# An attention and mixture-of-experts kernel on one core: output weights in eight pieces, a third query buffer, and late loads on ScalarE's queue

## Chip, cores and metric

The kernel runs on 1 core of one Trainium2 chip. The metric is the device time of one execution in microseconds, the median of three runs. Engines are named as the profile names them: PE (matrix products), DVE (VectorE), ACT (ScalarE), POOL (GpSimd) and SP (SyncE, which here only issues DMAs).

## What is computed

One layer for 2048 rows of 256 features: attention with 16 heads of 128 and weights stored as codes and block scales, then a mixture of 8 experts of width 176, two of them chosen for each row. Cut to what matters:

```
x = x + layernorm(attention(layernorm(x)))
x = x + layernorm(experts(layernorm(x)))

attention(x): w  = codes * repeat(scales, 32)          # for wq, wk, wv, wo
              q, k, v = x @ wq + bq, x @ wk + bk, x @ wv + bv
              out = softmax(q k^T / sqrt(128)) v       # each of 16 heads, 2048 x 2048
              return out @ wo + bo
experts(x):   top 2 of softmax(x @ Wr), weights normalised
              sum over them of weight * ((silu(x @ Wg) * (x @ Wu)) @ Wd)
```

## The kernel before, in words

All engines run one instruction list each, in the order in which the Python code calls them (a manual schedule); nothing is reordered. Numbers are held as a 16-bit high part and a low part, so most products run as three.

**The main loop** (L832 to L889) runs over 256 tiles `g`, 16 tiles `t` of 128 query rows for each of 16 heads `h`. In a tile, PE makes the scores of 128 queries with 2048 keys in two halves `s` (L511 to L515, 12 matmuls of 512 columns), DVE takes their maxima (`m`, L516, and L520), ACT the exponentials (`p`, L527). One tile later ACT scales `p` to the high part `ph` (L541) and SP issues its transpose by DMA to `pth`; DVE makes the low part `pl` in two halves (L556), one of them two tiles later, and SP issues the transpose to `ptl`. PE multiplies the transposed parts with `v` in units of 6 matmuls (`pv`, L582), two units a tile, 13 units behind. After eight units ACT, POOL and POOL's DMA queue write a block of 512 queries to the scratch `ot_d` in HBM (L597 to L602).

**Filling work** (`fill`, L610) puts projections into the tiles: a block of q or k in even tiles, v in odd ones. PE writes them to the single PSUM buffer `pj`, ACT copies them out (L246, L277), POOL splits them in two parts (L247, L248, L278, L279). In the first six tiles of head 0 the v blocks of the first pair of heads use the buffer `pv` and are split by ACT and DVE (L269, L270). A q block serves four tiles; it lies in a buffer `qT` of which there are 2. In the last head the three remaining q blocks are made at tiles 0, 1 and 2, the last two into slots of the pool (`qT_l`).

**One pool of slots.** `NX = 21` slots of 4 KB a partition under the tag `x` hold `ph`, `pl`, the k and v tiles, the raw and finished output weights, attention output read back (`oi`), raw expert weights (`gu_raw`, `draw`), inputs (`x1`) and more. A tile takes the slot that was given up first, and whoever writes it first waits until its last reader is done; for `pl` that is the DMA of its transpose.

**Output weights.** Codes (`woc`) and scales (`wos`) come in four pieces each before the loop. `dequant_wo` (L637) multiplies one piece on POOL in each of tiles 0 to 3 of head 0 (L642, 128x1024). The results `wo` are first read in head 14.

**The last two heads.** `early` (head 14, L793) prepares the bias row (`crow`, `brow`, which share one slot) and begins to load `oi`. `late` (head 15, L810) does the first rows' output product: `OI_LOAD` names the tiles at which an `oi` is loaded, `OI_USE` those at which its 16 matmuls (L727) run; `GW_LOAD` and `GW_SPLIT` do so for the four pieces of the experts' gate weights, which ACT and POOL split (L661, L663). All these loads are issued on SP's queue, between the transposes. The gate weights' buffer takes the place of the projections' input and weights, so it is opened once the last projection is emitted.

**After the loop** (L1107 on) the last `pv` units, the rest of the first output products (`op_mm`, L712), layer norms, routing and then the experts run, a block of 512 rows after the other.

Of the kernel before, what the change touches and what calls it, by code (L numbers as in the profile page):

```python
# [8 lines left out]
F32 = mybir.dt.float32  # L9
F32R = mybir.dt.float32r  # L10
BF = mybir.dt.bfloat16
HP = mybir.dt.float16
# [3 lines left out]
ALU = mybir.AluOpType  # L16
# [5 lines left out]
D = 256  # L22
# [11 lines left out]
NX = 21  # L34
# [3 lines left out]
def sandwich(  # L38
# [22 lines left out]
    nc = tc.nc  # L61
# [45 lines left out]
    small = ctx.enter_context(tc.tile_pool(name="small", bufs=4))  # L107
# [85 lines left out]
    kqv = ctx.enter_context(tc.tile_pool(name="kqv", bufs=2))  # L193
# [20 lines left out]

    def kq_tile(which, h, b):
        if which == "q":
            return kqv.tile([128, 2, 512], HP, name="qT", bufs=2)
        if b % 2 == 0:
            KP[h] = kqv.tile([128, 2, 2, 512], HP, name="kT", tag="x", bufs=NX)
        return KP[h][:, b % 2]  # L220

    def proj_qk(which, h, b, tag="pj", wide=None, slot=None):
        w = W[(h // 2, which)]
        bias = bqs[:, IX[which], h : h + 1]
        ps = proj_psum(tag)
        col = bass.ts(h % 2, 128)
        n = 0
        for kc in range(2):
            for hl in range(2):
                nc.tensor.matmul(  # L230
                    ps, w[:, kc, col], xnT[:, 4 * b : 4 * b + 4, hl * 2 + kc, :],
                    start=(n == 0), stop=(n == 3),
                )
                n += 1
        if slot is None:
            t = kq_tile(which, h, b)
        else:
            t = kqv.tile([128, 2, 512], HP, name="qT_l", tag="x", bufs=NX)
        if wide is None:
            nc.scalar.activation(t[:, 0, :], ps, AF.Identity, bias=bias)  # L240
            pending.append(lambda: nc.vector.scalar_tensor_tensor(
                t[:, 1, :], ps, bias, t[:, 0, :], ALU.add, ALU.subtract
            ))
        else:
            t32 = wide.tile([128, 512], F32, name="t32")
            nc.scalar.activation(t32, ps, AF.Identity, bias=bias)  # L246
            nc.gpsimd.tensor_copy(t[:, 0, :], t32)  # L247
            nc.gpsimd.tensor_tensor(t[:, 1, :], t32, t[:, 0, :], ALU.subtract)  # L248
        (Q if which == "q" else K)[(h, b)] = t
# [31 lines left out]
    wo = []  # L281
    wo_raw = {}
# [291 lines left out]
    def pv_part(h, b, e):  # L574
# [11 lines left out]
        if e == 7:  # L586
# [20 lines left out]
    QK = {0: ("q", 0, 1), 2: ("k", 1, 0), 4: ("q", 0, 2), 6: ("k", 1, 1),  # L607
          8: ("q", 0, 3), 10: ("k", 1, 2), 12: ("q", 1, 0), 14: ("k", 1, 3)}

    def fill(h, t):  # L610
        p = h // 2
        if h == 0 and t < 6:
            proj_v(0, 4 + 2 * t, 2, "pv")
        if h == NH - 1:
            if t < 3:
                proj_qk("q", h, t + 1, wide=soft, slot="x" if t > 0 else None)
        elif t in QK:
            kind, dh, b = QK[t]
            if h + dh < NH:
                proj_qk(kind, h + dh, b, wide=soft)  # L620
        elif h % 2 == 0:
            if t in (3, 5) and h > 0:
                proj_v(p, 12 + (t - 3) // 2, 1, wide=soft)
            elif t == 7 and h > 0:
                proj_v(p, 14, 2, wide=soft)
            elif t >= 9 and p + 1 < NH // 2:
                proj_v(p + 1, (t - 9) // 2, 1, wide=soft)
        elif p + 1 < NH // 2:
            proj_v(p + 1, 4 + t // 2, 1, wide=soft)
# [4 lines left out]
            pv_part(n // 4, n % 4, e)  # L634


    def dequant_wo(q):  # L637
        sc, cd = wo_raw.pop(q)
        if q % 2 == 0:
            wo.append(kqv.tile([128, 8, D], BF, name="wo", tag="x", bufs=NX))  # L640
        hs = slice(4 * (q % 2), 4 * (q % 2) + 4)
        nc.gpsimd.tensor_tensor(wo[q // 2][:, hs], cd, sc, ALU.mult)  # L642

    def bias_row():
        pb = psA.tile([128, 512], F32, name="pb", tag="pj")
# [21 lines left out]
    def load_gu(src, i, pool, tag, bufs, eng=None):  # L667
        kc, eh = divmod(i, 2)
        stg = pool.tile([128, 4, I], F32, name="gu_raw", tag=tag, bufs=bufs)
        (eng or nc.sync).dma_start(  # L670
            out=stg,
            in_=src.rearrange("e (kc p) i -> kc p e i", p=128)[kc][:, 4 * eh : 4 * eh + 4],
        )
        return stg
# [11 lines left out]
    def load_oi(b, half, j, tag="x", eng=None):  # L686
        oi = kqv.tile(
            [128, 4, 2, 256], HP, name="oi", tag=tag, bufs=NX
        )
        (eng or nc.sync).dma_start(  # L690
            out=oi.rearrange("p h l q -> p (h l q)"),
            in_=ot_d[b][:, half, 4 * j : 4 * j + 4].rearrange("p h l q -> p (h l q)"),
        )
        OIN[(b, half, j)] = oi
# [82 lines left out]
    def ln_c(b):  # L777
# [1 line left out]

    X1 = {}  # L780
    XV = x.rearrange("b (c p t) d -> p (b c) t d", p=128, t=4)
    GW_LOAD = {0: 1, 3: 2, 5: 3}
    GW_SPLIT = {4: 0, 6: 1, 8: 2, 10: 3}
    OI_LOAD = {
        2: (0, 1, 0), 4: (0, 1, 1), 6: (0, 1, 2), 9: (1, 0, 0), 10: (1, 0, 1),
        12: (0, 0, 3), 13: (0, 1, 3), 14: (1, 0, 2),
    }
    OI_USE = {
        4: (0, (0,)), 5: (0, (1,)), 6: (0, (2,)), 8: (1, (0,)), 9: (1, (1,)), 10: (1, (2,)),
        14: (0, (3,)), 15: (1, (3,)),  # L790
    }

    def early(t):  # L793
        nonlocal crow, brow
        if t == 7:
            cb = kqv.tile([128, 2, D], F32, name="crow", tag="x", bufs=NX)
            crow, brow = cb[:, 0], cb[:, 1]
            nc.sync.dma_start(out=brow, in_=bo.partition_broadcast(128))
        if t == 9:
            gst["b3"] = bias_row()  # L800
        if t == 11:
            bias_row2(gst.pop("b3"))
        if t == 13:
            nc.gpsimd.tensor_tensor(crow, crow, brow, ALU.add)
        if t in (8, 10, 12):
            load_oi(0, 0, t // 2 - 4)
        if t == 14:
            gst[0] = load_gu(wg, 0, kqv, "x", NX)

    def late(t):  # L810
        nonlocal gw
        if t == 3:
            proj_ctx.close()
            rp = ctx.enter_context(tc.tile_pool(name="gw", bufs=1, side="right"))
            gw = rp.tile([128, 2, 2, NCH, 128], F32R)
        if t in OI_USE:
            op_mm(0, *OI_USE[t], "pj", 2)
        if t in GW_SPLIT:
            split_gu(gw, GW_SPLIT[t], gst.pop(GW_SPLIT[t]), True)
        if t in GW_LOAD:  # L820
            i = GW_LOAD[t]
            gst[i] = load_gu(wg, i, kqv, "x", NX)
        if t in OI_LOAD:
            load_oi(*OI_LOAD[t])
        if t == 8:
            X1[0] = kqv.tile([128, 4, D], F32, name="x1_0", tag="x", bufs=NX)
            nc.sync.dma_start(out=X1[0], in_=XV[:, 0])


    defer = False  # L830
# [1 line left out]
    for g in range(NS + 2):  # L832
        h, t = divmod(g, NT)
        live = g < NS
        if live:
            m = small.tile([128, 8], F32, name="m", bufs=6)
            s0 = scores_half(h, t, 0, m)
            if g == 0:
                proj_v(0, 0, 2)
                proj_v(0, 2, 2, "pv")  # L840
        if prev is not None:
            recip(prev[2])
        if prev2 is not None:
            low_half(1, *prev2)
        flush()
        if defer:
            pv_unit(2 * g - 1)
            defer = False
        pv_unit(2 * g)
        if prev is not None:  # L850
            prev = (*prev, high_part(*prev))
        if live:
            s1 = scores_half(h, t, 1, m)
            negmax(m)
            p = softmax((s0, s1), m)
        if prev is not None:
            low_half(0, *prev)
        prev2 = prev
        first = live and (2 * g + 1 - PVLAG) % 8 == 0
        if not first:  # L860
            pv_unit(2 * g + 1)
        if live:
            fill(h, t)
        if first and h == NH - 1:
            defer = True
        elif first:
            pv_unit(2 * g + 1)
        if live:
            prev = (h, t, m, p)
        else:  # L870
            prev = None
        if live:
            weight_steps(h, t)
        if h == 0 and t in (8, 9):
            tail_consts(t - 8)
        if g < 4:
            dequant_wo(g)
        if h == NH - 2:
            early(t)
        if h == NH - 1:  # L880
            late(t)
        if g == NS:
            ln_a(0)
        if g == NS + 1:
            load_oi(1, 0, 3)
            ust = [load_gu(wu, 0, kqv, "x", NX)]
            ust += [load_gu(wu, i, kqv, "x", NX) for i in range(1, 4)]
            ln_b1(0)
# [222 lines left out]
    uw = uwp.tile([128, 2, 2, NCH, 128], F32R)  # L1111
    d0 = load_d(0)
    d1 = load_d(4)
    op_mm(1, 0, (0, 1), "s")
    ln_b2(0)
    split_gu(uw, 0, ust[0], True)
    ln_c(0)
# [2 lines left out]
    tr(0, 0, "s")  # L1120
    tr(0, 1, "s")
    split_gu(uw, 1, ust[1], False)
    op_mm(1, 0, (2, 3), "s")
    for j in range(4):
        load_oi(1, 1, j)
    router_a(0, "s")
# [112 lines left out]
```

## Time and profile before

| | |
|---|---|
| three runs | 1839.41, 1842.27, 1844.51 us; median 1842.27 |
| profiled execution | 1839.29 us, span 1837.5 us |
| granted clock of PE, mean | 0.990 |
| PE, DVE, ACT, POOL busy | 1780.7, 1635.1, 1371.9, 943.3 us |
| transposes issued by SP | 2 x 256, median 2.2 us (`pth`) and 3.0 us (`ptl`) each |
| main loop | about 36 to 1566 us |
| output weight products on POOL (L642) | 4 of 2.36 us, from 41.6 us on |

Times in the profile are from the start of the span. A timeline row gives start, duration, engine, line, operation, output<-inputs and shapes; in brackets stands how long the engine was idle before it and what ended that wait. A row of one line's instructions gives their number, then the shortest, median and longest duration in ns, and when the first and last began. A matmul of 512 columns starts every 0.22 us when PE runs at its full clock, though each shows 0.38 us. SP's rows are the issuing of a DMA, not its transfer.

### The profile page before, as it was taken

The numbers are of one execution on the slowest core, as the hardware profiler recorded it, in microseconds if no ns is written. First come the engines' busy times: TensorE is split into PE (matmuls) and PEld (weight loads), VectorE is DVE, ScalarE is ACT, GpSimd is POOL, SyncE is SP. The second block draws the span as 40 slices with busy tenths as digits, with TensorE's granted clock in tenths as the row PEclk, the third lists the DMA queues.
The fourth block names the chain that finished last, engine by engine and source line by source line (L and its number), as shares of the span: only waits on it lengthen the run. The fifth ranks groups of instructions, "written<-read, shape, count | busy, mean of one in ns | idle before, by whom it ended". The sixth has DMA issues, their size and how long they took to land. (4 is left out here: it accounts for less than half of the span.)

```text
span 1837.5 us, 25510 instructions
## 1 busy us (share of the span) xinstructions
PE 1780.7 (97%) x8890; PEld 936.4 (51%) x8890; DVE 1635.1 (89%) x2269; ACT 1371.9 (75%) x1732; POOL 943.3 (51%) x911
## 2 busy tenths in 40 slices
PE   7699999999999999999999999999999999899997
PEld 4344444444444444444444444444444444588886
DVE  7899999999999999999999999999999978558665
ACT  5688888888888888888888888888888877322232
POOL 3456556565656565656565656566444332323232
PEclk9899999999999999999999999999999999999999
DMA  7799999999999999999999999999999999921000
GB/s 172 136 196 203 199 199 199 203 202 189 200 207 193 201 198 208 194 200 198 199 199 198 204 205 202 194 205 198 191 190 194 216 217 227 310 83 35 1 13 23
DMA packets 1092336, 330.70 MB, mean 180 GB/s; under 512 B 1069728, under 2 KB 1079280, under 8 KB 1092208
## 3 DMA queue, kind: packets, MB, share of 16 engines
q1 hardware_dynamic: 1081744, 301.02, 89.8%
q0 software_dynamic: 9920, 27.82, 5.7%
q8 instruction: 70, 1.15, 0.2%
q14 instruction: 58, 0.48, 0.1%
q10 hardware_dynamic: 544, 0.23, 0.0%
HBM read 41.68 MB, written 18.87 MB: 33 GB/s over the span
## 5 line engine op out<-in xcount | busy, mean ns | idle before, releaser
L527 ACT ACTIVATE p<-s,m,ssc 128x1024 f32<-128x1024 f32 x512 | 612.2, 1200 | 182.7 <-DVE m L520 176.0
L556 DVE SCALAR_TENSOR_TENSOR pl<-p,m,ph 128x1024 f16<-128x1024 f32 x512 | 730.3, 1426 | 9.1 <-ACT ph L541 7.0
L516 DVE TENSOR_REDUCE m<-s 128x1 f32<-128x1024 f32 x512 | 622.0, 1215 | 37.1 <-PE s L515 34.9
L541 ACT ACTIVATE ph<-p,m 128x2048 f16<-128x2048 f32 x256 | 512.8, 2003 | 62.3 <-ACT t L246 17.3
L582 PE MATMUL pv<-pth,v 128*128 128x512 f16 x2048 | 506.3, 380 | 10.5 <-issue 5.1
L582 PEld LDWEIGHTS <-v 128*128 128x128 f16 x3072 | 301.0, 98 | 378.1 <-issue 10.0
L511 PE MATMUL s<-kT,qT 128*128 128x512 f16 x992 | 377.3, 380 | 5.9 <-ACT p L527 5.2
L512 PE MATMUL s<-kT,qT 128*128 128x512 f16 x992 | 377.2, 380 | 0.0
L515 PE MATMUL s<-kT,qT 128*128 128x512 f16 x992 | 296.0, 380 | 0.0
L582 PE MATMUL pv<-ptl,v 128*128 128x512 f16 x1024 | 253.1, 380 | 0.0
L247 POOL CAST qT<-t 128x512 f16<-128x512 f32 x61 | 76.4, 1252 | 231.7 <-ACT t L246 231.7
L278 POOL CAST v<-t 128x256 f16<-128x256 f32 (+1 forms) x105 | 44.0, 419 | 256.8 <-ACT t L277 256.8
L279 POOL TENSOR_TENSOR v<-t,v 128x256 f16<-128x256 f32 (+1 forms) x105 | 163.0, 1552 | 8.5
L515 PEld LDWEIGHTS <-qT 128*128 128x128 f16 x992 | 97.3, 98 | 118.0 <-issue 1.6
L512 PEld LDWEIGHTS <-qT 128*128 128x128 f16 x992 | 97.3, 98 | 114.0 <-issue 11.6
L511 PEld LDWEIGHTS <-qT 128*128 128x128 f16 x992 | 97.3, 98 | 106.3 <-issue 2.2
L1004 POOL TENSOR_TENSOR hh<-sg,hh 128x512 fp32r<-128x512 f32 x42 | 55.1, 1311 | 143.4 <-ACT hh L1003 108.4
L1003 ACT CAST hh<-sg 128x512 fp32r<-128x512 f32 (+1 forms) x45 | 27.5, 611 | 107.1 <-DVE sg L1015 107.0
L527 ACT ACTIVATION_READ_ACCUMULATOR p<-s,m,ssc 128x1 f32 x512 | 99.0, 193 | 0.0
L599 POOL TENSOR_TENSOR o<-t,o 128x512 f16<-128x512 f32 x63 | 93.6, 1486 | 5.2
L247 POOL CAST kT<-t 128x512 f16<-128x512 f32 x60 | 64.8, 1080 | 60.3 <-ACT t L246 56.5
L258 PE MATMUL pj<-wv,xnT 128*128 128x256 bf16 x512 | 75.9, 277 | 16.2 <-DVE v L270 16.1
(197 smaller groups left out, 1894.7 us busy)
## 6 DMA issues: line engine op xcount, KB each, us to landing
oi<-ot_d SPq DMA_DIRECT2D x32, 512.0 KB, 5.5
ot_d<-o POOLq DMA_DIRECT2D x63, 256.0 KB, 4.5
pth<-ph SPq DMA_TRANSPOSE x256, 5.1
ptl<-pl SPq DMA_TRANSPOSE x256, 5.4
xt<-in_L_attn_x SPq DMA_DIRECT2D x4, 512.0 KB, 4.2
woc<-in_L_attn_wo_codes SPq DMA_DIRECT2D x4, 512.0 KB, 8.7
wos<-in_L_attn_wo_scales SPq DMA_DIRECT2D x16, 128.0 KB, 8.1
x<-in_L_attn_x SPq DMA_DIRECT2D x4, 512.0 KB, 5.0
```

The source lines that it names most:

```text
L247: nc.gpsimd.tensor_copy(t[:, 0, :], t32)
L258: nc.tensor.matmul(ps[:, bass.ts(j, 256)], xnT[:, t0 + j, hl * 2 + kc, :], w[:, kc, :], start=(i == 0), stop=(i == 3),)
L279: nc.gpsimd.tensor_tensor(v[:, 1, sl, :], t32, v[:, 0, sl, :], ALU.subtract)
L511: nc.tensor.matmul(s[:, j, :], q[:, 0, qc], k[:, 0, :], start=True, stop=False)
L512: nc.tensor.matmul(s[:, j, :], q[:, 0, qc], k[:, 1, :], start=False, stop=False)
L515: nc.tensor.matmul(s[:, j, :], q[:, 1, qc], k[:, 0, :], start=False, stop=True)
L516: nc.vector.tensor_reduce(m[:, half : half + 1], s, AX.XY, ALU.max)
L527: nc.scalar.activation(p[:, bass.ts(i, 1024)], s, AF.Exp, bias=m[:, 2:3], scale=ssc[:, 0:1], accum_out=m[:, 3 + i : 4 + i],)
L541: nc.scalar.activation(ph, p, AF.Copy, scale=m[:, 6:7])
L556: nc.vector.scalar_tensor_tensor(pl[:, cs], p[:, cs], m[:, 6:7], ph[:, cs], ALU.mult, ALU.subtract)
L582: nc.tensor.matmul(ps, V[(h // 2, c // 4)][:, i % 2, c % 4, dc], d[:, :, c, :], start=(n == 0), stop=(n == 47),)
L599: nc.gpsimd.tensor_tensor(o[:, :, 1, :], halves(t32), o[:, :, 0, :], ALU.subtract)
```

## The change

- `dequant_wo` works in eight pieces of half the size, one in each of tiles 7 to 14 of head 0.
- `qT` has three buffers. In the last head the q blocks are made at tiles 0, 1 and 4, all in `qT`; `qT_l` is gone.
- `crow` moves to a buffer of its own in the pool `small`; `brow` alone takes a slot of `x`.
- The loads of `oi` in heads 14 and 15, of the gate weights and of `x1_0` are issued on ACT's queue, sixteen in all. The first gate piece is loaded in head 15 at tile 2 and no longer in head 14; in head 15 there is one load in each of tiles 2 to 14.
- In head 15 the gate buffer is opened at tile 5 instead of 3; the gate splits and the first three output products come one tile later.
- After the loop, three of four parts of an output product run ahead of the next `pv` units instead of two.

```diff
-            return kqv.tile([128, 2, 512], HP, name="qT", bufs=2)
+            return kqv.tile([128, 2, 512], HP, name="qT", bufs=3)
...
-        if slot is None:
-            t = kq_tile(which, h, b)
-        else:
-            t = kqv.tile([128, 2, 512], HP, name="qT_l", tag="x", bufs=NX)
+        t = kq_tile(which, h, b)
...
+    LASTQ = {0: 1, 1: 2, 4: 3}
...
-            if t < 3:
-                proj_qk("q", h, t + 1, wide=soft, slot="x" if t > 0 else None)
+            if t in LASTQ:
+                proj_qk("q", h, LASTQ[t], wide=soft)
...
-    def dequant_wo(q):
-        sc, cd = wo_raw.pop(q)
-        if q % 2 == 0:
+    def dequant_wo(j):
+        sc, cd = wo_raw[j // 2]
+        if j % 4 == 0:
             wo.append(kqv.tile([128, 8, D], BF, name="wo", tag="x", bufs=NX))
-        hs = slice(4 * (q % 2), 4 * (q % 2) + 4)
-        nc.gpsimd.tensor_tensor(wo[q // 2][:, hs], cd, sc, ALU.mult)
+        hs = slice(2 * (j % 4), 2 * (j % 4) + 2)
+        rs = slice(2 * (j % 2), 2 * (j % 2) + 2)
+        nc.gpsimd.tensor_tensor(wo[j // 4][:, hs], cd[:, rs], sc[:, rs], ALU.mult)
...
-    GW_LOAD = {0: 1, 3: 2, 5: 3}
-    GW_SPLIT = {4: 0, 6: 1, 8: 2, 10: 3}
+    GW_LOAD = {2: 0, 4: 1, 6: 2, 8: 3}
+    GW_SPLIT = {5: 0, 7: 1, 9: 2, 11: 3}
     OI_LOAD = {
-        2: (0, 1, 0), 4: (0, 1, 1), 6: (0, 1, 2), 9: (1, 0, 0), 10: (1, 0, 1),
+        3: (0, 1, 0), 5: (0, 1, 1), 7: (0, 1, 2), 9: (1, 0, 0), 10: (1, 0, 1),
         12: (0, 0, 3), 13: (0, 1, 3), 14: (1, 0, 2),
     }
     OI_USE = {
-        4: (0, (0,)), 5: (0, (1,)), 6: (0, (2,)), 8: (1, (0,)), 9: (1, (1,)), 10: (1, (2,)),
+        5: (0, (0,)), 6: (0, (1,)), 7: (0, (2,)), 8: (1, (0,)), 9: (1, (1,)), 10: (1, (2,)),
...
-            cb = kqv.tile([128, 2, D], F32, name="crow", tag="x", bufs=NX)
-            crow, brow = cb[:, 0], cb[:, 1]
+            crow = small.tile([128, D], F32, name="crow", bufs=1)
+            brow = kqv.tile([128, D], F32, name="brow", tag="x", bufs=NX)
...
         if t in (8, 10, 12):
-            load_oi(0, 0, t // 2 - 4)
-        if t == 14:
-            gst[0] = load_gu(wg, 0, kqv, "x", NX)
+            load_oi(0, 0, t // 2 - 4, eng=nc.scalar)
...
-        if t == 3:
+        if t == 5:
             proj_ctx.close()
...
-            gst[i] = load_gu(wg, i, kqv, "x", NX)
+            gst[i] = load_gu(wg, i, kqv, "x", NX, nc.scalar)
         if t in OI_LOAD:
-            load_oi(*OI_LOAD[t])
-        if t == 8:
+            load_oi(*OI_LOAD[t], eng=nc.scalar)
+        if t == 11:
             X1[0] = kqv.tile([128, 4, D], F32, name="x1_0", tag="x", bufs=NX)
-            nc.sync.dma_start(out=X1[0], in_=XV[:, 0])
+            nc.scalar.dma_start(out=X1[0], in_=XV[:, 0])
...
-        if g < 4:
-            dequant_wo(g)
+        if 7 <= g < 15:
+            dequant_wo(g - 7)
...
-    op_mm(1, 0, (0, 1), "s")
+    op_mm(1, 0, (0, 1, 2), "s")
...
-    op_mm(1, 0, (2, 3), "s")
+    op_mm(1, 0, (3,), "s")
```

More of the change, by code (lines that the diff above doesn't have):

```diff
@@ L220, in kq_tile, with proj_qk @@
         return KP[h][:, b % 2]
-    def proj_qk(which, h, b, tag="pj", wide=None, slot=None):
+    def proj_qk(which, h, b, tag="pj", wide=None):
         w = W[(h // 2, which)]
```

## The prediction

> **What bounds the kernel now.** The page first: span and busy shares.
>
> ```profile
> span 1837.5 us, 25510 instructions
> ...
> PE 1780.7 (97%) x8890; PEld 936.4 (51%) x8890; DVE 1635.1 (89%) x2269; ACT 1371.9 (75%) x1732; POOL 943.3 (51%) x911
> ```
>
> PE at 97% of the whole span hides where it is not busy, so next the busy times by stage: the first six tiles, a whole head, and two stretches of the last head (columns: length, then busy us of PE, PEld, DVE, ACT, POOL, then the granted clock, the DMA share and GB/s).
>
> ```profile
> 36.00:80.00 44.00, 26.95 (x119) 12.69 (x118) 36.41 (x41) 28.78 (x37) 20.91 (x18) 0.85 0.60 105
> ...
> 143.00:237.00 94.00, 93.77 (x451) 43.90 (x449) 90.45 (x114) 79.78 (x100) 55.63 (x56) 1.00 1.11 200
> ...
> 1476.00:1508.00 32.00, 27.95 (x143) 14.35 (x141) 21.30 (x27) 21.14 (x24) 8.55 (x6) 0.89 1.11 216
> 1508.00:1560.00 52.00, 50.18 (x272) 26.28 (x270) 46.47 (x63) 40.95 (x46) 14.10 (x10) 1.00 1.12 228
> ```
>
> A head in the middle is bound by PE (93.8 of 94 us), with DVE close behind (90.5). Nothing the change touches can shorten that. PE is idle in two places: 17 of the 44 us at the start, at a granted clock of 0.85, and some 4 of 32 us in the last head, at 0.89. The timeline of the start says why.
>
> ```profile
> 41.64 2.35 POOL L642 TENSOR_TENSOR wo<-woc,wos 128x1024 bf16<-128x1024 f32 x1
> ...
> 41.70 3.38 DVE L556 SCALAR_TENSOR_TENSOR pl<-p,m,ph 128x1024 f16<-128x1024 f32 x1 [0.17 <-ACT ph L541]
> ...
> 49.80 1.89 PE L258 MATMUL pj<-wv,xnT 128*128 128x256 bf16 x8 [5.38 <-DVE v L270]
> ...
> 58.43 4.67 POOL L642 TENSOR_TENSOR wo<-woc,wos 128x1024 bf16<-128x1024 f32 x2
> ...
> 59.86 4.34 DVE L556 SCALAR_TENSOR_TENSOR pl<-p,m,ph 128x1024 f16<-128x1024 f32 x1
> ```
>
> DVE's `pl` (1.27 us undisturbed) ends only about 1.1 us after POOL's weight product does: it stands still while POOL runs. PE then waits for DVE, and after such a gap the eight matmuls take 1.89 us instead of 1.05 (the row at 58.47). In the last head the ACT and PE timelines show the second place:
>
> ```profile
> 1485.72 2.00 ACT L541 ACTIVATE ph<-p,m 128x2048 f16<-128x2048 f32 x1 [7.47 <-DMA ptl<-pl]
> ```
>
> ```profile
> 1488.96 0.58 PE L511 MATMUL s<-kT,qT 128*128 128x512 f16 x1 [4.05 <-ACT p L527]
> ...
> 1491.47 2.68 PE L582 MATMUL pv<-ptl,v 128*128 128x512 f16 x6
> ```
>
> `ph` waits for the slot of an older `pl`, whose transpose is still under way: the pool's 21 slots are used up. Two more PE waits follow:
>
> ```profile
> 1550.19 1.92 PE L727 MATMUL op<-wo,oi 128*128 128x256 bf16 x16 [1.75 <-DMA oi<-ot_d]
> ...
> 1575.44 7.22 PE L582 MATMUL pv<-pth,v 128*128 128x512 f16 x24 [5.14 <-issue]
> ```
>
> **Part 1, the weight product leaves tiles 0 to 3.** The three stretched `pl` lose 3.38, 2.71 and 4.34 less 1.27 each: 2.1 + 1.4 + 3.1 = 6.6 us. They are on the path: at this point each tile is a chain, v product on PE, scores, DVE maximum, `pl`, v split on DVE, next v product. Undisturbed, its terms give 0.06 + 0.9 + 1.5 + 1.1 + 0.4 + 1.3 + 0.65 = 5.9 us, and 0.9 more on a tile with a k or q projection. From one v split's end to the next, five tiles took 9.7, 8.7, 9.0, 8.7 and 6.7 us, together 42.8, against 3 x 5.9 + 2 x 6.8 = 31.3. Of the 11.5 over, 6.6 are the stretches and about 4.7 the slow clock after PE's gaps (1.89 + 1.91 us for 1.05 + 1.03 is one such case). POOL's other products stay (`pl` at 1.5 and 1.8 us), and whether the clock holds with gaps of 2.5 us is open: one gap of 2.37 us kept it, one of 2.67 us was followed by slow matmuls. Bounds 5 to 11; I take 8.0.
>
> **The eight halves in tiles 7 to 14.** On POOL they cost 8 x 1.27 (the 128x512 product at L184) beside 35 us busy of 63, so POOL itself bears it; behind each in its queue stand the casts of the next tile, needed four tiles later. The question is DVE, 96% busy there. The Trainium skill (SBUF — State Buffer, Who interferes with whom) has a DVE instruction with two SBUF inputs and a GpSimd instruction reading SBUF exclude each other for the whole instruction, so by the rule eight pieces could take up to 8 x 1.2 = 9.6 us of DVE: the harm is moved, not removed. The row for the middle heads is milder: POOL has a product of this size in most tiles there, and the median `pl` is 1.42 against 1.27, some 0.3 us a tile, since POOL as often is the one that waits (L248 alternates 1.16 and 2.01). That gives 2.4 us, less DVE's slack of about 0.2 us a tile: 1.0 lost. I take the row; range 0 to 9.6. The eight raw tiles now hold slots until tile 14: up to 18 of 21 in tiles 4 to 11 by my count, the next one free having been released two tiles (11 us) before, longer than a transpose takes to land (5.4). No wait, taken as 0.
>
> **Part 2, slots in the last head.** Live at the stalled `ph`: 2 output weights, the bias tile, 2 k, 4 v, 2 late q, 3 raw gate pieces, 4 `oi`, and one `ph`, before `pl` and `at` want theirs. The change takes out both q tiles, the bias tile (`crow` lives elsewhere, `brow` is done at tile 13) and two gate pieces not yet loaded: at most 17 of 21 at any time, by the same count. The stall goes: 4.05 us of PE plus 6 score and 6 pv matmuls at about 0.43 us instead of 0.22, 12 x 0.21 = 2.5: 6.5. What is late next is PE itself: the last head's other tiles already ran at PE's 6.9 us (with output product) or DVE's 5.6, and the same number of each remains. The third query buffer costs nothing that runs; moving one projection from tile 2 to 4 leaves it eight tiles before use.
>
> The 1.75 us wait for `oi`: its load was issued at 1544.85 behind two transposes on SP, 5.2 us after the tile's maximum; on ACT it comes behind the tile's exponentials, about 2.5 us after it. It lands about when PE arrives: 1.5 gained.
>
> **Part 3, sixteen loads on ACT.** Three in head 14, thirteen in head 15, one a tile from 2 to 14. Behind each on ACT stands the next `ph`, then the exponentials; SP loses the same sixteen issues, of no value as such, since it is not waited for elsewhere. No load's slot or source is recent (each was released two tiles or more before), so the waits are nothing; the issue is the cost. Rows that are near:
>
> ```profile
> 1.34 0.37 ACTq L297 DMA_DIRECT2D smax<-in_L_attn_wq_scales  x1
> ```
>
> ```profile
> L690 SPq DMA_DIRECT2D oi<-ot_d x11: 423/858/1270, 1413.6 to 1558.9; - x11
> ```
>
> ```profile
> L562 SPq DMA_TRANSPOSE ptl<-pl x256: 1317/3016/4972, 49.3 to 1572.1; - x128
> ```
>
> ACT issues in about 0.4 us when nothing else does, SP in 0.86 amid its transposes. Against it: the Trainium skill (Perfetto Trace Analysis, DMA Instruction — HWDGE) says that the descriptor generator is shared by both issuing sequencers and locked until one DMA's descriptors are made. SP is issuing transposes for 256 x (2.2 + 3.0) of some 1530 us, 88%, so by the rule an ACT issue finds it locked and waits half a transpose: 0.4 + 1.2 = 1.6 us on the mean, 5.4 at worst. ACT's slack is (52 - 40.95) / 9 = 1.2 us a tile in the last head and about 1.0 in head 14, much of it just before `ph` (0.5 to 0.7 us). By the row all is hidden; by the rule 16 x 0.5 = 8 us. I take about 0.9 us an issue, nearer the row: 1.5 us lost in tiles that also split a gate piece (1.44 us). Range 0 to 16 x 1.5 = 24.
>
> **Part 4, the tail.** PE idles 5.14 us until the last transposes land; one `oi`'s 16 matmuls (half of the 3.5 us at 1566) move into that gap and leave the full stretch behind: 1.75 gained; the gap has 3.4 left. The four loads waiting for those slots on SP only come earlier.
>
> **Sum.** 8.0 - 1.0 + 6.5 + 1.5 - 1.5 + 1.75 = 15.25 us. The profiled execution took 1839.3 (span 1837.5 and 1.8 around it), so 1824.0; it is 3.0 below the median of the three runs, and against that 1842.3 the same gain gives 1827.0.
>
> **Rivals.** *ACT's issue is the new bound* (slower). One mechanism: the lock above, at every one of the 16 loads. The rest of the sum is 16.75 us, or 1.05 a load over 1.1 slack: from about 2.1 us an issue nothing is left, and at 2.8, nearly a whole transpose, 16 x 1.7 = 27 makes 1842.3 - 16.75 + 27 = 1852. For it: SP issues 88% of the time. Against: SP's own loads, amid that traffic, took at most 1.27. *The product's harm is only moved* (small gain): the eight halves cost 6 to 9 and the slow clock stays at the start (5 instead of 8): 15.25 - 3 - 6 = 6, 1836. Against: the median `pl`. *The stall comes back* elsewhere in the last head, as a wait of ACT for a slot or of PE for a later `oi`: 15.25 - 6.5 - 1.5 = 7, 1835. Against: four slots free by count.
>
> **Chances.** The forecast 0.62, with 0.04 more for a larger gain (every bound at its best, 22 us, 1820); moved harm 0.13; stall back 0.09; slower 0.12. A difference under 0.3% (5.5 us) can't be told from none here. The two middle rivals lie around that limit, half on each side: faster 0.77, same 0.11, slower 0.12. Range 1818 to 1843: it takes in both middle rivals and leaves out the slow one and the extreme.
>
> **What would show it.** Right: no `pl` over 2.5 us in the first tiles; the first six tiles 8 us shorter; no ACT wait on a `ptl` transpose in the last head; output product without the 1.75; the gap before the last pv at 3.4. Wrong: ACT-queue issues over 2 us each, with PE waiting for `p`; `pl` stretched in tiles 7 to 14; slow matmuls still at 67 to 80 us.

## The result, and the profile after

The changed kernel takes 1825.57 us (median of four runs, 1824.03 to 1829.47) against 1841.74 us for the kernel before (four runs): a ratio of 0.9915, 95% interval 0.9894 to 0.9936, or 16.2 us less. The forecast was 15.25 us less. As will be seen, the total came out right by luck: the part at the start brought more than forecast and the rest less, and the two errors nearly cancel.

The profiled execution is the slowest of the four, 1829.47 us, while the profile of before (1839.29 us) lies just below its three timed runs. So the two spans differ by only 9.9 us, and a part of the 16.2 us isn't in these two profiles. The page after:

```profile
span 1827.6 us, 25508 instructions
...
PE 1775.5 (97%) x8890; PEld 934.1 (51%) x8890; DVE 1631.0 (89%) x2269; ACT 1371.5 (75%) x1732; POOL 946.9 (52%) x915
```

PE's busy share is the same 97%, so the page alone says nothing of where the time went. The busy times of the four stretches that were shown of before, moved to where the same work now stands (columns: length, busy us of PE, PEld, DVE, ACT, POOL, granted clock, DMA share, GB/s), say more:

```profile
36.00:80.00 44.00, 32.65 (x159) 15.40 (x158) 38.48 (x53) 36.17 (x45) 14.81 (x16) 0.96 0.78 144
134.00:228.00 94.00, 94.00 (x453) 44.18 (x452) 90.59 (x113) 80.07 (x101) 57.97 (x60) 1.00 1.13 198
1469.00:1501.00 32.00, 32.00 (x180) 17.39 (x179) 27.52 (x36) 26.87 (x31) 13.10 (x8) 1.00 1.14 235
1501.00:1553.00 52.00, 45.23 (x234) 22.76 (x232) 40.91 (x55) 35.25 (x41) 12.08 (x9) 0.97 1.13 228
```

At the start PE has 32.65 us of work in 44 instead of 26.95, at a clock of 0.96 instead of 0.85. A head in the middle is bound by PE as it was (94.00 of 94 us). The first stretch of the last head is now full (32 of 32; it was 27.95). But the second has got worse: 45.23 of 52 instead of 50.18. The idle time has moved there.

DVE's timeline of the first tiles shows the start mended; no `pl` up to 80 us takes more than 1.50 us any more:

```profile
41.79 1.28 DVE L553 SCALAR_TENSOR_TENSOR pl<-p,m,ph 128x1024 f16<-128x1024 f32 x1 [0.17 <-ACT ph L538]
44.56 1.26 DVE L553 SCALAR_TENSOR_TENSOR pl<-p,m,ph 128x1024 f16<-128x1024 f32 x1
47.78 1.28 DVE L553 SCALAR_TENSOR_TENSOR pl<-p,m,ph 128x1024 f16<-128x1024 f32 x1
...
58.62 1.26 DVE L553 SCALAR_TENSOR_TENSOR pl<-p,m,ph 128x1024 f16<-128x1024 f32 x1
```

Measured from one tile's negated maximum (DVE, L520 before and L517 after) to the next, tiles 0 to 5 took 48.1 us and now take 38.5; tiles 6 to 15, which the eight halves now share, took 58.9 and take 59.1. That is 9.3 us less, nearly all of the 9.9 us by which the spans differ. The 14 heads between took 1315.2 us and take 1317.5, and from the last head's first tile to the end the time falls by 3.0. (Those 14 heads take 1315.2 to 1316.4 us in the three profiles with the old slots and 1316.7 to 1321.5 in the eleven with the new ones; the cause stays open.)

PE's timeline of the last head shows where the idle time went (in brackets the wait and what ended it):

```profile
1536.24 1.92 PE L727 MATMUL op<-wo,oi 128*128 128x256 bf16 x16 [0.85 <-DMA oi<-ot_d]
...
1545.06 4.31 PE L579 MATMUL pv<-pth,v 128*128 128x512 f16 x12 [5.60 <-DMA pth<-ph]
...
1567.83 7.03 PE L579 MATMUL pv<-pth,v 128*128 128x512 f16 x24 [2.41 <-issue]
```

ACT's wait for a slot, which cost PE 4.05 us, is gone, but in tile 14 PE waits 5.60 us for a transposed piece of `ph`; the 12 matmuls behind it take 4.31 us, where 12 in the same head take 2.75 undisturbed. From its tile 0 to its tile 15 the last head took 100.5 us and takes 100.8. SP's timeline shows the transposes falling behind ahead of that wait:

```profile
1519.89 4.98 SPq L541 DMA_TRANSPOSE pth<-ph  x1
1524.97 4.17 SPq L559 DMA_TRANSPOSE ptl<-pl  x1
1529.23 6.72 SPq L541 DMA_TRANSPOSE pth<-ph  x1
```

The medians of all issues are 2.3 us (`pth`) and 2.9 us (`ptl`). By the trace these three landed 10.5, 11.4 and 9.6 us after their issue began; the median of all is 5.1 (`pth`) and 5.3 (`ptl`). The work after the last tile took 278.9 us and takes 275.6.

### The profile page after: what moved, and what is told of

It reads as the page before. It is cut to its first block, busy times and chain, and to the rows that moved or that the text cites. A ratio compares the mean times of both kernels' runs of the same rounds, so it can differ in the third digit from the quotient of the medians.

```text
span 1827.6 us, 25508 instructions
## 1 busy us (share of the span) xinstructions
PE 1775.5 (97%) x8890; PEld 934.1 (51%) x8890; DVE 1631.0 (89%) x2269; ACT 1371.5 (75%) x1732; POOL 946.9 (52%) x915
## 5 line engine op out<-in xcount | busy, mean ns | idle before, releaser
L508 PE MATMUL s<-kT,qT 128*128 128x512 f16 x1024 | 388.5, 379 | 2.7 <-ACT p L524 2.0
L509 PE MATMUL s<-kT,qT 128*128 128x512 f16 x1024 | 388.6, 379 | 0.7 <-POOL kT L245 0.7
L512 PE MATMUL s<-kT,qT 128*128 128x512 f16 x1024 | 304.6, 379 | 0.0
L512 PEld LDWEIGHTS <-qT 128*128 128x128 f16 x1024 | 100.3, 98 | 122.0 <-issue 1.5
L509 PEld LDWEIGHTS <-qT 128*128 128x128 f16 x1024 | 100.2, 98 | 113.7 <-issue 7.5
L508 PEld LDWEIGHTS <-qT 128*128 128x128 f16 x1024 | 100.3, 98 | 109.0 <-issue 1.0
L1001 ACT CAST hh<-sg 128x512 fp32r<-128x512 f32 (+1 forms) x45 | 27.5, 612 | 107.0 <-DVE sg L1013 107.0
L245 POOL TENSOR_TENSOR kT<-t,kT 128x512 f16<-128x512 f32 x60 | 89.8, 1496 | 5.1
```

What stands on the lines that cost most here:

```text
L508: nc.tensor.matmul(s[:, j, :], q[:, 0, qc], k[:, 0, :], start=True, stop=False)
L509: nc.tensor.matmul(s[:, j, :], q[:, 0, qc], k[:, 1, :], start=False, stop=False)
L512: nc.tensor.matmul(s[:, j, :], q[:, 1, qc], k[:, 0, :], start=False, stop=True)
```

## Experiments

Each ran in at least four executions beside the kernel before. Ratios are to it; in the four sets of runs its median was 1842.0 to 1843.5 us. A short name stands for each kernel. Where differences from the changed kernel count, the ratios are subtracted, once from that of the changed kernel (0.9915) and once from that of its repetition below (0.991): 0.001 is 1.84 us. Each ratio has an interval of some 3 us to either side (1.7 for *no pieces*), so a difference of less than about 4 us between two changed kernels can't be told from none by their times alone. Profiles are of single executions.

**Which part brings how much.** *Pieces only* is the kernel before with the new `dequant_wo` in tiles 7 to 14 and nothing else.

```diff
-        if g < 4:
-            dequant_wo(g)
+        if 7 <= g < 15:
+            dequant_wo(g - 7)
```

> The kernel before with only the output weight product moved: eight halves in tiles 7 to 14 of head 0. The theory from the two traces: the first six tiles lose their stretched pl and slow matmuls and the later tiles pay nothing, so about 9.5 us below the kernel before (1832). The prediction's sum had 8.0 less 1.0, so 7.0 below (1834.7). Rival, the harm is only moved: 3 below or less. In the trace: tiles 0 to 5 at 38 to 39 us instead of 48, tiles 6 to 15 unchanged at 59; by the prediction 40 and 60; by the rival tiles 6 to 15 at 65 or more.

1831.77 us, ratio 0.9934 (0.9919 to 0.995): 12.2 us less, 9.2 to 14.9 by the interval, which takes in the theory's 9.5 but neither the prediction's 7.0 nor the rival's 3. Tiles 0 to 5 take 39.4 us, tiles 6 to 15 take 59.1: the later tiles pay next to nothing.

*No pieces* is the changed kernel with the product back in tiles 0 to 3 (the same edit, reversed).

> The changed kernel with the output weight product put back (four whole pieces in tiles 0 to 3): the last two heads and the tail alone. The prediction's sum for these parts is 6.5 + 1.5 - 1.5 + 1.75 = 8.25 below the kernel before (1833.5). The theory from the one trace of the changed kernel: the last head gives back what it gains as a wait of PE for pth transposes, so only the tail's 3 us are left (1838.7). In the trace: the last head 8 us shorter than 100.5 by the first, 100 or more by the second, with a PE wait of over 4 us on a pth transpose.

1837.14 us, ratio 0.9968 (0.9959 to 0.9977): 5.9 us less (4.2 to 7.6), between the two expectations, 8.25 and 3. In its profiled execution (1844.35 us, the slowest of its nineteen) the last head took 103.5 us, and PE waited twice in tile 14, for an `oi` and for a `pth` transpose:

```profile
1550.49 3.59 PE L726 MATMUL op<-wo,oi 128*128 128x256 bf16 x16 [4.11 <-DMA oi<-ot_d]
...
1559.10 4.44 PE L579 MATMUL pv<-pth,v 128*128 128x512 f16 x12 [2.57 <-DMA pth<-ph]
```

The second expectation had one wait of over 4 us for `pth`; here it is split in two, and the time is lower than it had it. The two parts add up: 12.2 + 5.9 = 18 against some 16 for the whole change, within their intervals. Its profile also shows how hard the start can be hit. On DVE's timeline:

```profile
56.50 7.15 DVE L553 SCALAR_TENSOR_TENSOR pl<-p,m,ph 128x1024 f16<-128x1024 f32 x1
63.57 0.68 DVE L267 TENSOR_TENSOR v<-pj,v 128x512 f16<-128x512 f32 x1
```

and on POOL's:

```profile
57.91 4.65 POOL L641 TENSOR_TENSOR wo<-woc,wos 128x1024 bf16<-128x1024 f32 x2
```

Two products stand back to back, because the first was held up behind a k split and DMA issues, and `pl` ends 1.1 us after the second. That tile takes 15.0 us. In the profile of the kernel before, the same product cost less (its longest `pl` took 4.34 us), so its start may have been a mild one; no typical execution of before was profiled.

**Was the wait in tile 14 an accident?** *Again* is the changed kernel, unchanged.

> The changed kernel a second time, unchanged, for a second profile and five more executions. If the 5.6 us wait of PE for a pth transpose in tile 14 of the last head belongs to the schedule, it is there again and the profiled execution lies at the median of its runs; if it is an event of one execution, it is absent, the last head takes 95 us or less and the profiled execution lies near 1824.

1827.44 us, ratio 0.991 (0.9895 to 0.9925), last head 100.1 us, and on PE's timeline

```profile
1546.09 4.97 PE L579 MATMUL pv<-pth,v 128*128 128x512 f16 x12 [5.25 <-DMA pth<-ph]
```

The wait belongs to the schedule; three kernels below that keep these loads have it in tile 14 too (4.45 us in *whole late*, 5.27 in *half early*, 3.54 in *tail back*). The profiled execution is again the slowest of its set (1829.70), not at the median as expected; why, stays open.

**The place of the product, or its size?** *Whole late* has the four whole pieces in tiles 7, 9, 11 and 13; *half early* the eight halves in tiles 0 to 7.

```diff
-        if 7 <= g < 15:
-            dequant_wo(g - 7)
+        if g in (7, 9, 11, 13):          # whole late, with the old dequant_wo
+            dequant_wo((g - 7) // 2)
+        if g < 8:                        # half early
+            dequant_wo(g)
```

> The changed kernel with the output weight product in its four whole pieces (128x1024, 2.36 us each), one in each of tiles 7, 9, 11 and 13 of head 0. Theory place: what cost the time was the place, tiles 0 to 5, where each tile is one chain through DVE and PE then falls to its slow clock; later PE works on queued pv units and a stopped DVE costs little: within 1.5 us of the changed kernel (1826 to 1829), tiles 6 to 15 at 59 to 60 us. Rival size: a whole piece stops DVE for up to 2.4 us wherever it stands, and the halves are what helps: 4 pieces of about 2 us less the slack of DVE, 4 to 8 us above the changed kernel (1831 to 1835), with pl over 3 us in tiles 7 to 14.

> The changed kernel with the eight halves in tiles 0 to 7 of head 0 instead of 7 to 14. Theory place: the first tiles stretch again, each half stops pl by up to 1.2 us and two that queue up behind one another by 2.4, so 5 to 9 us above the changed kernel (1832 to 1836), tiles 0 to 5 at 43 to 47 us. Rival size: a half is short enough to fit between DVE's two-input instructions, within 2 us of the changed kernel (1825 to 1829), tiles 0 to 5 at 39 to 40 us.

Whole late: 1830.9 us, ratio 0.9933 (0.9916 to 0.9949), 3 to 4 us above the changed kernel, at the edge of what the times can tell. Half early: 1833.43 us, ratio 0.9947 (0.9931 to 0.9963), 6 to 7 us above. So the place counts, and the size seems to. The profiles, for tiles 0 to 15 together:

| head 0, us | tiles 0 on | tiles 7 on |
|---|---|---|
| whole pieces | 107.0 (before), 109.4 (no pieces) | 101.8 |
| halves | 100.9 | 97.6 (changed), 98.5 (again) |

A row of each on DVE's timeline and the piece on POOL's at the same moment, whole late first and half early second:

```profile
111.33 3.64 DVE L553 SCALAR_TENSOR_TENSOR pl<-p,m,ph 128x1024 f16<-128x1024 f32 x1
...
111.51 2.37 POOL L641 TENSOR_TENSOR wo<-woc,wos 128x1024 bf16<-128x1024 f32 x1
```

```profile
41.22 1.27 POOL L642 TENSOR_TENSOR wo<-woc,wos 128x512 bf16<-128x512 f32 x1
...
41.27 2.29 DVE L553 SCALAR_TENSOR_TENSOR pl<-p,m,ph 128x1024 f16<-128x1024 f32 x1 [0.17 <-ACT ph L538]
```

The first is 1.27 us of work plus the whole length of the piece, the second 1.27 us plus 1.0 of the 1.27. So in these rows a piece stops DVE for about as long as it runs, in either place. Late, PE has `pv` units queued and works on: behind the row of 3.64 us its timeline has no gap up to 118 us, while behind the row of 2.29 us it waits 3.22 us for DVE (1.97 at the same place in the changed kernel). Tiles 6 to 15 of whole late lose 3.3 us in all, for four pieces that early cost 9.5 and more. Neither theory alone holds.

**ScalarE's queue.** *SP queue* is the changed kernel with all sixteen loads on SP at the same tiles.

```diff
-            load_oi(*OI_LOAD[t], eng=nc.scalar)
+            load_oi(*OI_LOAD[t])
...
-            nc.scalar.dma_start(out=X1[0], in_=XV[:, 0])
+            nc.sync.dma_start(out=X1[0], in_=XV[:, 0])
```

> The changed kernel with all sixteen loads on SyncE's queue, at the same tiles. Theory: the issues on ScalarE (0.33 to 0.42 us in the changed kernel's trace) are hidden, and a load in the transposes' own queue only delays them; the slots are what matters: within 2 us of the changed kernel (1824 to 1828), with perhaps one wait for an oi in the output product. Rival A, ScalarE's issues cost: 3 to 8 us below the changed kernel (1818 to 1823). Rival B, the second queue brings the loads forward and this is what removes waits: 4 us or more above the changed kernel (1830 or more). Rival C, a load in a queue of its own takes the DMA engines from the transposes and makes the 5.6 us wait for pth in the last head: that wait is gone here and the last head is 5 us shorter than 100.8.

1827.2 us, ratio 0.9908 (0.9891 to 0.9925): no difference from the changed kernel that the times can tell. PE waits in tile 14, but for something else:

```profile
1545.79 3.59 PE L727 MATMUL op<-wo,oi 128*128 128x256 bf16 x16 [8.38 <-DMA oi<-ot_d]
```

An `oi` that stands behind the late transposes is late with them. The last head takes 103.5 us, but the work after it 271.5, which fits transposes that caught up while PE waited. None of the rivals A to C holds by time: the queue moves PE's wait from a transpose to a load, and neither the 3 us gain of A nor the 4 us loss of B is seen, nor the shorter head of C.

**Bytes.** *More loads* adds four loads that nobody reads; *half bytes* loads two of four heads for eleven `oi` (`n` is 2 for these). Its output products take those two heads twice, so all engines have the same work, and the attention output of the other two is left out of the result.

```diff
+        if t in (0, 1, 2, 3):            # more loads
+            xtra = kqv.tile([128, 4, 2, 256], HP, name="xtra", tag="x", bufs=NX)
+            nc.scalar.dma_start(
...
-            in_=ot_d[b][:, half, 4 * j : 4 * j + 4].rearrange("p h l q -> p (h l q)"),
+            in_=ot_d[b][:, half, 4 * j : 4 * j + n].rearrange("p h l q -> p (h l q)"),
```

> The changed kernel with four more loads of 512 KB on ScalarE's queue in tiles 0 to 3 of the last head, into slots that nothing reads. Theory DMA: in the last head the transposes and the loads together fill the DMA engines (22 to 23 MB in 100 to 103 us at 221 to 228 GB/s in every kernel so far), and what comes on top is carried to the wait for pth in tile 14: 2.1 MB at 225 GB/s are 9 us, less what drains by then, so 4 to 9 us above the changed kernel (1831 to 1836) and the wait of 5.6 us at 10 or more. Rival burst: the wait is made by the loads of tiles 9 to 13 and a slow read of x alone; loads in tiles 0 to 3 are gone by then, within 2 us of the changed kernel. Rival issue: ScalarE's issues cost, at 0.4 us each 1.6 us at most.

> The changed kernel with the eleven loads of attention output in heads 14 and 15 at half their size (two of four heads each); the output products take those two heads twice, so the other half of that attention output is left out of the result and all engines have the same work. Theory DMA: 2.1 MB less in the last head, 9 us of its DMA time, so the wait for pth in tile 14 is gone, the last head takes 94 to 95 us by PE instead of 100.8, and the time is 5 to 8 us below the changed kernel (1818 to 1821). Rival: the wait comes from the order or the latency of the transposes, not from bytes: it stays at 4 us or more and the time within 2 us.

More loads: 1835.52 us, ratio 0.9953 (0.9936 to 0.9969), 7 to 8 us above the changed kernel, as the theory had it (4 to 9); the rival of a mere burst, within 2 us, fails. The last head takes 105.6 us; in this execution head 2 was slow as well (97.7 us), which the loads can't explain. The expectation had the wait in tile 14 grow. It didn't; a new one came in tile 6, the first row here:

```profile
1494.39 4.36 PE L579 MATMUL pv<-pth,v 128*128 128x512 f16 x12 [2.92 <-ACT p L524]
...
1552.09 5.06 PE L579 MATMUL pv<-pth,v 128*128 128x512 f16 x12 [5.13 <-DMA pth<-ph]
```

That row names ACT's `p`, which had ended 0.9 us before; by the trace a `pth` transpose landed at 1494.30, just ahead of PE's start. So this wait too was for a transpose, as was one of 2.6 us in head 2 of this execution, which ended as a `pth` landed.

Half bytes: 1822.57 us, ratio 0.9885 (0.9866 to 0.9904), some 5 us below the changed kernel, at the lower end of what was expected. The last head takes 93.8 us, tile 14 takes 7.1 us instead of 14.1, and PE has no wait over 0.4 us in it; the rival, by which the wait stays, fails. The last head of before, of the changed kernel and of half bytes, in the columns of above:

```profile
1458.11:1558.59 100.48, 94.61 (x483) 47.50 (x481) 82.91 (x110) 76.81 (x88) 33.04 (x24) 0.97 1.12 221
```

```profile
1451.20:1551.96 100.76, 93.99 (x483) 47.34 (x482) 84.39 (x110) 76.75 (x88) 33.97 (x24) 0.98 1.15 228
```

```profile
1450.72:1544.55 93.83, 93.19 (x492) 47.88 (x490) 84.27 (x110) 76.88 (x88) 34.72 (x24) 1.00 1.12 219
```

PE has the same 93 to 95 us of work in all three. What differs is the data: 100.48 us at 221 GB/s are 22.2 MB, 100.76 at 228 are 23.0, 93.83 at 219 are 20.5; a head in the middle moves 94 at 198, 18.6 MB. It isn't the number of packets: the whole of half bytes has 1,092,336 and the changed kernel 1,092,337. The DMA share is about 1.1 in all of these heads, with PE waiting or not, so it alone doesn't tell them apart. That 13 full loads on top of the transposes don't fit into one head is read from the bytes, and from what adding and halving them did; whether the limit is the 16 engines themselves isn't shown.

**Slots or bytes?** *Old slots, half bytes* is pieces only with the same eleven loads halved: old buffers, old tiles, SP's queue.

> The kernel before with the product in halves in tiles 7 to 14 and with the same eleven loads of attention output at half their size (the other half of that attention output is left out, as in the earlier run with half bytes), but with the old slots, the old tiles of the loads and all loads on SyncE's queue. Theory one bound: the wait for a slot in tiles 3 and 4 of the last head was itself a transposed piece that landed late because the DMA engines were full, so with fewer bytes it is gone or small without any change to the slots: last head 94 to 96 us, time within 2 us of the run with half bytes (1821 to 1825). Rival slots: 20 of 21 slots taken make ph wait for a transpose issued in the tile before, whatever the bytes: ACT waits 4 us or more for a ptl transpose in tiles 3 to 5, last head 99 us or more, time 1827 to 1830.

1824.88 us, ratio 0.9904 (0.9888 to 0.992), last head 97.6 us. ACT's timeline:

```profile
1476.53 2.00 ACT L541 ACTIVATE ph<-p,m 128x2048 f16<-128x2048 f32 x1 [5.96 <-DMA ptl<-pl]
```

The slot wait is there with half the bytes, as the rival had it, so slots do make it, as the prediction said. But the time is that of the first theory. Against the same half loads with everything else of the change (*half bytes, SP queue*, the last run below) the last head is 1.8 us longer (97.6 against 95.8) and the time some 3 us by ratio, within the intervals. No wait over 0.5 us came in tile 14; that the transposes caught up while PE stood still for the slot fits this, but isn't shown alone.

**The loads spread, the same bytes.**

```diff
-    GW_LOAD = {2: 0, 4: 1, 6: 2, 8: 3}
+    GW_LOAD = {2: 0, 6: 2, 8: 3}         # piece 1: head 14, tile 7
...
-        3: (0, 1, 0), 5: (0, 1, 1), 7: (0, 1, 2), 9: (1, 0, 0), 10: (1, 0, 1),
+        1: (0, 1, 0), 7: (0, 1, 2),      # (0,1,1): head 14, tile 9; (1,0,0), (1,0,1): tile 15
...
-        if t == 11:
+        if t == 9:
             X1[0] = kqv.tile([128, 4, D], F32, name="x1_0", tag="x", bufs=NX)
```

> The changed kernel with its loads spread, the same bytes in all: one gate piece and one oi moved into head 14 (tiles 7 and 9), one oi from tile 3 to 1 of the last head, x from tile 11 to 9, and the two oi that only the end needs from tiles 9 and 10 to tile 15. Theory DMA: tiles 10 and 11 are free of loads and the queue has drained when the last block of transposes is due, so the 5.6 us wait in tile 14 and the slow matmuls behind it (1.5 us) go; some 2 to 3 us come back ahead of the last pv units, where two loads were added: 3 to 5 us below the changed kernel (1821 to 1824). Rival: the bytes are only moved to another wait (ahead of the last pv units, or a slot that is not yet free in tiles 5 to 8), within 1.5 us of the changed kernel.

1828.25 us, ratio 0.9918 (0.9903 to 0.9933): no gain, the rival holds. The wait in tile 14 is gone and the last head takes 94.4 us, but the work after it takes 282.1, with new waits for loads and transposes. On PE's timeline:

```profile
1557.19 1.92 PE L727 MATMUL op_s<-wo,oi 128*128 128x256 bf16 x16 [1.35 <-DMA oi<-ot_d]
1560.15 3.67 PE L727 MATMUL op_s<-wo,oi 128*128 128x256 bf16 x32 [1.04 <-DMA oi<-ot_d]
1570.75 7.71 PE L579 MATMUL pv<-pth,v 128*128 128x512 f16 x24 [6.93 <-DMA pth<-ph]
```

**The tail.** *Tail back* has the old order after the loop.

```diff
-    op_mm(1, 0, (0, 1, 2), "s")
+    op_mm(1, 0, (0, 1), "s")
...
-    op_mm(1, 0, (3,), "s")
+    op_mm(1, 0, (2, 3), "s")
```

> The changed kernel with the order after the loop as it was: two parts of the output product ahead of the last pv units instead of three. The prediction's term: 1.75 us above the changed kernel (about 1828), with the gap ahead of the last pv units 1.7 us longer than the changed kernel's 2.4 (about 4.1) and the output product's rows 32 and 32 matmuls instead of 48 and 16. Rival: the part that is moved is hidden anyway, because what follows waits for something else: no difference, within 1 us.

1826.87 us, ratio 0.9918 (0.9904 to 0.9932), 0.6 to 1.5 us above the changed kernel: the times can't tell the term of 1.75 from nothing. With 32 matmuls ahead of it instead of 48, the gap is

```profile
1563.29 7.03 PE L579 MATMUL pv<-pth,v 128*128 128x512 f16 x24 [2.50 <-issue]
```

and not 4.1, though the changed kernel had 2.41. In *again*, with the new order, it is

```profile
1567.82 5.34 PE L579 MATMUL pv<-pth,v 128*128 128x512 f16 x24 [0.70 <-issue]
```

and in *pieces only*, with the old order, 2.70 us. So the gap differs from one execution of the same kernel to the next by as much as the term was worth, and the 5.14 us of before was the longest of these. What sets it isn't shown: with half the bytes it was 3.94 us.

**The queue without the full DMA engines.** *Half bytes, SP queue* has the sixteen loads of half bytes on SP.

> The run with half bytes (eleven loads of attention output at half their size in heads 14 and 15, the other half left out of the result) with all sixteen loads on SyncE's queue instead of ScalarE's. With the DMA engines relieved, the difference between the two is what the queue itself is worth. By the prediction's two terms that touch it, ScalarE's issues cost 1.5 us and an oi that comes earlier gains 1.5: no difference, 1821 to 1824.5. Rival A, ScalarE's issues cost (0.33 to 0.42 us each, 16 of them, none hidden): 4 to 6 us faster than the run with half bytes. Rival B, an oi behind transposes comes late: PE waits for an oi in tile 14 as it did for 8.4 us with full bytes on SyncE's queue; 2 us or more slower (1824.6 or more), with that wait in the trace.

1823.22 us, ratio 0.9887 (0.9871 to 0.9904): no difference in time. The trace shows rival B's wait, though, and a last head of 95.8 us instead of 93.8:

```profile
1539.05 1.92 PE L730 MATMUL op<-wo,oi 128*128 128x256 bf16 x16 [3.41 <-DMA oi<-ot_d]
```

So ScalarE's queue does bring an `oi` sooner. Whether that is worth 2 us or nothing, the times (0.4 us apart by ratio, some 3 us of interval each) can't tell.

All last heads and what follows them, from the profiles (single executions; two of the changed kernel differ by 2.2 us in the sum):

| kernel | last head, us | after it, us | sum |
|---|---|---|---|
| before; pieces only | 100.5; 103.6 | 278.9; 276.2 | 379.4; 379.8 |
| changed; again | 100.8; 100.1 | 275.6; 274.1 | 376.4; 374.2 |
| no pieces (its slowest execution) | 103.5 | 276.4 | 379.9 |
| whole late; half early | 99.7; 100.2 | 273.7; 277.0 | 373.4; 377.2 |
| SP queue | 103.5 | 271.5 | 374.9 |
| spread | 94.4 | 282.1 | 376.5 |
| tail back | 99.0 | 275.6 | 374.6 |
| more loads | 105.6 | 274.0 | 379.6 |
| half bytes; on SP | 93.8; 95.8 | 275.7; 276.0 | 369.5; 371.8 |
| old slots, half bytes | 97.6 | 274.7 | 372.3 |

Schedules with the same bytes and the new slots have a sum of 373 to 377 us, with one at 379.9, however the waits are placed; the two with the old slots have 379.4 and 379.8. With half the bytes it is 369.5 and 371.8, and 372.3 with the old slots.

## Why the prediction was right, and where its steps were not

**The start, 8.0, less 1.0 for the halves.** The mechanism is right and the size too small. By profile it is 9.5 us in tiles 0 to 5 and 0.2 lost in tiles 6 to 15; by time 12.2 alone and some 10 within the change. Three terms were mis-sized. The start itself was probably read from a mild execution (stretches of 2.1 + 1.4 + 3.1 us; no pieces had one of 5.9). More of the slow clock went than was taken: of PE's three gaps of 2.13 us in the changed kernel's first tiles, two leave it fast. And the halves cost 0.2 and not 1.0. There the row was the better guide than the rule of the Trainium skill (SBUF — State Buffer, Who interferes with whom), from which the prediction had estimated up to 9.6 for eight halves. For a single `pl` the rule is what one sees: 2.29 and 3.64 us with a piece at the same moment, 7.15 with two in a row. For the sum it is not: where PE has work queued, a stopped DVE costs less (four whole pieces 3.3 us late, 9.5 and more early).

**The slot stall, 6.5.** This step failed. "What is late next is PE itself" was wrong: late next were the transposes by DMA. The wait for a slot went, as foreseen, and 5.25 to 5.60 us of wait plus 1.6 of slow matmuls came in tile 14. The last head gained nothing in the changed kernel's profile; across the others with all these loads in it and new slots it took 99.0 to 103.5 us, against 100.5 and 103.6 with the old slots. What did come through shows only with the work after the head: the sum is 3.0 to 5.6 us lower in the changed kernel's two profiles than in the two with the old slots and full loads. The prediction had rows that hint at it on its table, 216 to 228 GB/s in the last head against 200 in a middle one, at a DMA share that was already 1.11, and read them as background. The third rival, the stall back as another wait in the last head, named the place and the kind (with PE waiting for an `oi`, which is what happened on SP's queue); it gave it 9 in 100, because it counted slots and not bytes.

**The `oi` wait, 1.5, and ScalarE's issues, -1.5.** The wait of 1.75 us became 0.85. The issues cost nothing that can be measured:

```profile
L690 ACTq DMA_DIRECT2D oi<-ot_d x11: 326/327/357, 1404.0 to 1541.9; - x11
```

```profile
L670 ACTq DMA_DIRECT2D gu_raw<-in_L_ffn_Wg x4: 393/412/417, 1463.0 to 1501.4; - x4
```

(shortest, median, longest in ns). They even run inside an exponential that is under way, on ACT's timeline of the changed kernel:

```profile
1494.45 1.19 ACT L524 ACTIVATE p<-s,m,ssc 128x1024 f32<-128x1024 f32 x1
1494.83 0.33 ACTq L690 DMA_DIRECT2D oi<-ot_d  x1
```

The lock of the descriptor generator, which the Trainium skill has (Perfetto Trace Analysis, DMA Instruction — HWDGE) and on which the slow rival stood, doesn't show in any of them, though SP was issuing transposes at the time of each; moving the loads to SP changed the time by nothing that can be told, with full loads and with half. The nearest row, 0.37 us, was the answer, and the 0.9 taken was a compromise without need.

**The tail, 1.75.** Not seen, though the times don't exclude it. The gap was taken as a fixed 5.14 us to be filled; it was 2.50 and 2.70 us in two other kernels with the old order, and 2.41 and 0.70 in two executions of the changed one.

**The sum.** Parts 2 to 4 were to give 8.25 and gave 5.9 (4.2 to 7.6); part 1 was to give 7.0 and gave 10 to 12. That the two errors nearly cancel is luck. What the 5.9 consist of isn't settled: ScalarE's queue and the order after the loop, each taken back alone, changed nothing that the times can tell, which leaves the slots and the new tiles of the loads. These were tested only together (and with that order), and only with half the bytes, where they made 1.8 us in the last head and some 3 by time, within the intervals. Of the signs named ahead, those of the start were right (no `pl` over 2.5 us in the first tiles, six tiles 9.5 us shorter, the slow matmuls mostly gone). Three `pl` of 2.0 to 2.3 us in tiles 12 to 14 of head 0 were named as a sign of failure and weren't one. ACT's wait for a `ptl` transpose went too, without bringing the 6.5 us. The gap ahead of the last `pv` was to be 3.4 and was 2.41.

## What to carry to other kernels

Before a wait is taken off a stage, ask what else is nearly full there: while one engine waits, other queues can drain, and when the wait goes, the next one may show. Multiply GB/s by time for the stage and for its neighbours; here 22 MB against 18.6 at the same DMA share was the hint that transposes and loads together would be late in the last head. Moving the loads to another queue or to other tiles only moved the waits between the last head and the work after it; halving eleven loads shortened the two together by 5 to 7 us. Work on an engine that stops another belongs where PE, which waits for the stopped engine, has other work queued, and in small pieces.

## What the runs showed of the hardware

In the changed kernel a transpose by DMA landed in 5.1 us (`pth`) and 5.3 us (`ptl`) at the median, and three in a row in 10.5, 11.4 and 9.6 us while a read of `x` (8.1 us to land, 4.6 in the kernel before), an `oi` and a write of `ot_d` were under way. After the last of these transposes had landed, loads of 512 KB landed 1.3 us apart. Two products on POOL in a row, 4.65 us together, held one 1.27 us instruction of DVE for 7.15 us (*no pieces*). The issues of the sixteen loads on ACT's queue took 0.33 to 0.42 us each, while SP was issuing transposes. After a wait of 5.6 us PE ran 12 matmuls in 4.31 us instead of 2.75; after a gap of 2.13 us it once ran slow (a v product in 1.83 us instead of 1.05) and twice not, and in *again* it ran slow after 1.97 us and fast after 2.49.
